# Seven products ahead of the last image's gates, its last row's sum in another order, and its last stores on two queues

## The chip, the core and the metric

The kernel runs on one core of a Trainium2 chip. A core has five engines that run their own instruction streams and wait for one another through semaphores: TensorE (PE in the profile; its weight loads are PEld), VectorE (DVE), ScalarE (ACT), GpSimd (POOL) and SyncE (SP, which here only issues DMAs). The metric is the device time of one launch in microseconds (us). Three runs of the kernel before gave 1615.23, 1620.63 and 1624.31 us, a median of 1620.63 us.

## The reference: what is computed

The input x has 4 images of 32 channels, 128 x 128, float32.

- Layer 0 makes 128 channels of 4096 points out of every image, forms the 4096-wide attention matrix of normalised points, applies it, scales by gamma and adds the input.
- Layer 1 reads the result as 4096 tokens of 128 values per image. It adds a linear attention of 8 heads (all of it folds into one 128 x 128 matrix per image), and then a mixture of experts. That last part is what matters here:

```
p = softmax(x @ router_w + router_b)        # 8 experts
top_p, top_i = top_k(p, 2);  top_p /= sum(top_p)
out = sum over the two chosen experts of top_p * (x @ expert_w[e] + expert_b[e])
t = t + out
```

## The kernel before

**Images 0 to 2** are pipelined: while one image's attention matrix is made, layer 1 of the image before runs beside it. Their tokens are sorted by expert through DRAM, so that each token meets only its two experts. **The last image (b = 3)** has nothing to hide behind, and its layer 1 is done in `last_parts` (L1419 to L1538) without sorting: every token is multiplied by all 8 expert matrices, and a gate of 8 numbers per token, 6 of them zero, weighs the results.

**Tokens.** The 4096 tokens of an image lie as 32 tiles (KT = 32) of 128 tokens; below, "row k" is tile k. `normalise` (L758, ACT) makes row k's normalised tokens, four rows are turned by four TensorE transposes into one bank of PSUM (`transpose_tokens`, L987, transposes at L995), and ACT copies the bank back (L991). Row k can only be multiplied once its group of four is turned and copied.

**Products.** `product(k, h, bank)` (L1433) multiplies row k with experts 0 to 3 (h = 0) or 4 to 7 (h = 1): one 128 x 512 float32 product, which the profile shows as two matmul records of line L1434. Its result fills one bank of PSUM. `bank` (L1423) hands out five banks in turn (two of the pool ps_e, two of ps_g, one of ps_o); a product waits until the two readers of the bank's former content are done. Three more banks belong to `psum_t` (L97), which the transposes and the temporaries of the second half's gates use.

**Weighing and adding.** For each row, `scaled_sums` (L1370, DVE, L1376) multiplies the first experts' results with their gates and adds them up in `acc`, starting from the token itself; `scaled_rows` (L1381, ACT, L1390) writes the other experts' results, each times its gate, into `tmp`. `by_scalar(k)` (L1429) says how many of the eight experts ACT takes: 6 for k < 8, 5 for k < 14, then 4. `sum_rows` (L1395) adds `tmp` into `acc` two rows at a time, on POOL; for the last pair (rows 30 and 31) on DVE, at L1398, L1399 and L1402. `store(g)` (L1404) writes four rows with four DMAs, all issued by SP.

**Order.** The streams of PE, DVE, ACT and SP are written in program order by hand (`manual_schedule`). Ahead of the row loop at L1521 stand the router of the first 16 rows (`router_rows`), its gates (`route(0)`, ending at L978), the turning of rows 0 to 3, the four products of rows 0 and 1 (L1519) and the turning of rows 4 to 7 (L1520). In the loop, row k is weighed and the two products of row k + 2 are issued. The second half's statistics and gates (`second_half`, L1473) are spread over the loop's first passes.

Of the kernel before, what the change touches and what calls it, by code (L numbers as in the profile page):

```python
# [12 lines left out]
F32 = mybir.dt.float32  # L13
BF16 = mybir.dt.bfloat16
U32 = mybir.dt.uint32
AF = mybir.ActivationFunctionType
ALU = mybir.AluOpType
# [5 lines left out]
def kernel(  # L23
# [43 lines left out]
    nc = tc.nc  # L67
    P = 128
# [7 lines left out]
    KT = 32  # L76
    S = 32
    NH, KQ, D = wk.shape
# [10 lines left out]
    work = ctx.enter_context(tc.tile_pool(name="work", bufs=2))  # L89
# [7 lines left out]
    def psum_t(name):  # L97
        return ps_t.tile([P, CH], F32, tag="pt", name=name)
# [172 lines left out]
    def tokens(ap, b):  # L271
        return ap[b].rearrange("c (s k r) w -> s r c k w", s=2, r=2)
# [445 lines left out]
    def layer1(b, st):  # L718

        alone = b == B - 1  # L720
        T = st["T"]
# [9 lines left out]
        gate = first  # L731
# [155 lines left out]
        def matrix():  # L887

            nc.vector.reciprocal(sda, rsa)
            gv = work.tile([P, NH, D + E], F32, tag="wide", name=f"gv_{b}")  # L890
            for h0 in range(0, NH, 3):
                yield
                nh = min(3, NH - h0)
                dst = gv[:, h0 : h0 + nh].rearrange("p h e -> p (h e)")

                def copy(p, dst=dst, nh=nh, h0=h0):
                    if h0 == 3:
                        nc.scalar.activation(dst, p[:, : nh * (D + E)], AF.Copy)
                    else:
                        nc.vector.tensor_copy(dst, p[:, : nh * (D + E)])  # L900

                py, done = hold(f"pgv_{b}_{h0}", copy)
                rhs = wvx[:, h0 : h0 + nh].rearrange("p h e -> p (h e)")
                nc.tensor.matmul(py[:, : nh * (D + E)], gram, rhs, start=True, stop=True)
                yield
                done()
            yield
            pm, done = hold(f"pm_{b}", lambda p: nc.vector.tensor_copy(matx[:, : D + E], p[:, : D + E]))
            for h in range(NH):
                nc.tensor.matmul(pm[:, : D + E], at_sb[:, h, :], gv[:, h, :], start=(h == 0), stop=(h == NH - 1))  # L910
            yield
            done()
# [454 lines left out]
        dst = tokens(out, b)  # L1367
        accs, tmps = {}, {}
# [23 lines left out]
                    scale=gate[:, k, e : e + 1],  # L1392
                )

        def sum_rows(kk, n=4, eng=nc.gpsimd):  # L1395
            tmp, rows = tmps[kk], accs[kk // 2][:, 2 * (kk % 2) : 2 * (kk % 2) + 2, :]
            m = n // 2
            eng.tensor_tensor(tmp[:, :, :m], tmp[:, :, :m], tmp[:, :, m : 2 * m], ALU.add)  # L1398
            eng.tensor_tensor(tmp[:, :, 0], tmp[:, :, 0], tmp[:, :, 1], ALU.add)  # L1399
            if n >= 5:  # L1400
                eng.tensor_tensor(rows, rows, tmp[:, :, 2 if n == 6 else 4], ALU.add)
            eng.tensor_tensor(rows, rows, tmp[:, :, 0], ALU.add)  # L1402

        def store(g):  # L1404
            for r1 in range(2):
                for s in range(2):
                    p0 = s * 64 + r1 * 32
                    nc.sync.dma_start(dst[s, r1, :, ts(g, 4), :], accs[g][p0 : p0 + 32])

        def all_parts():  # L1410
            yield from stagger([close_rows(kc) for kc in range(4)], 3)
# [7 lines left out]
        def last_parts():  # L1419

            turn = [0]

            def bank(name):  # L1423
                pools = ((ps_e, "pe"), (ps_g, "pg"), (ps_o, "po"), (ps_e, "pe"), (ps_g, "pg"))
                pool, tag = pools[turn[0] % 5]
                turn[0] += 1
                return pool.tile([P, CH], F32, tag=tag, name=name)

            def by_scalar(k):  # L1429

                return 6 if k < 8 else 5 if k < 14 else 4

            def product(k, h, bank):  # L1433
                nc.tensor.matmul(bank, xn[:, k, :D], ew_sb[:, 4 * h : 4 * h + 4, :], start=True, stop=True)  # L1434
                return bank

            for _ in matrix():
                pass

            la = fpool.tile([P, KT, 2 * E], F32, tag="F", name=f"la_{b}")  # L1440
            copies = {}

            def attended(u):
                if u >= 2:
                    copies[u] = fpool.tile([P, 8, D], F32, tag="F", name=f"pac_{b}_{u}")
                for j0 in range(0, 8, 3):
                    pa = bank(f"pat_{b}_{u}_{j0}")
                    attend_rows(u, j0, pa)
                    nj = min(3, 8 - j0)
                    pr = pa[:, : nj * (D + 2 * E)].rearrange("p (j d) -> p j d", d=D + 2 * E)  # L1450
                    if u < 2:
                        tg = T[:, 8 * u + j0 : 8 * u + j0 + nj, :]
                        nc.vector.tensor_tensor(tg, tg, pr[:, :, :D], ALU.add)
                    else:
                        nc.scalar.activation(copies[u][:, j0 : j0 + nj], pr[:, :, :D], AF.Copy)
                    nc.scalar.activation(la[:, 8 * u + j0 : 8 * u + j0 + nj, :], pr[:, :, D:], AF.Copy)

            def stats_of(u):
                bs, stats = batch_stats("f", 8 * u, 8)
                for f in stats:  # L1460
                    f()
                close_stats("f", 8 * u, 8, bs)

            attended(0)
            stats_of(0)
            transpose_rows(6)()
            transpose_rows(7)()
            attended(1)
            stats_of(1)
            attended(2)  # L1470
            attended(3)

            def second_half():  # L1473

                bs, stats = batch_stats("f", 16, 16)
                for u in (2, 3):
                    tg = T[:, ts(u, 8), :]
                    nc.vector.tensor_tensor(tg, tg, copies[u], ALU.add)
                    yield
                    for j in range(8):  # L1480
                        stats[8 * u - 16 + j]()
                        if j % 4 == 3:
                            yield
                close_stats("f", 16, 16, bs)
                yield

                temps = psum_t("gates").rearrange("p (n k e) -> p n k e", n=4, e=E)
                logits = router_rows(nc.vector, 16, 16, la[:, 16:], temps)
                next(logits)
                yield  # L1490
                yield
                for _ in logits:
                    pass
                gates = route(1, temps)
                next(gates)
                yield
                for g in range(4, 8):
                    normalise(range(4 * g, 4 * g + 4), rsf, nbo)
                    next(gates, None)
                    yield  # L1500
                    transpose_tokens(g)()
                    yield

            rest = second_half()
            logits = router_rows(nc.vector, 0, 16, la[:, :16])
            next(logits)
            normalise(range(0, 4), rsf, nbo)
            keep_running(6)
            transpose_tokens(0)()
            next(rest)  # L1510
            for _ in logits:
                pass
            gates = route(0)
            normalise(range(4, 8), rsf, nbo)
            next(gates)
            next(rest)
            for _ in gates:
                pass
            products = [product(k, h, bank(f"py_{b}_{k}_{h}")) for k in range(2) for h in range(2)]  # L1519
            transpose_tokens(1)()  # L1520
            for k in range(KT + 4):  # L1521
                if k < KT:
                    n = by_scalar(k)
                    scaled_sums(k, products[:2], 8 - n)
                    scaled_rows(k, products[:2], n)
                    products = products[2:]
                    if k + 2 < KT:
                        products += [product(k + 2, h, bank(f"py_{b}_{k + 2}_{h}")) for h in range(2)]
                if 1 <= k <= KT and k % 2 == 0:
                    sum_rows(k // 2 - 1, by_scalar(k - 2), nc.vector if k == KT else nc.gpsimd)  # L1530
                if k >= 5 and k % 4 == 1:
                    store(k // 4 - 1)
                if k < 8:
                    normalise(range(8 + k, 9 + k), rsf, nbo)
                    if k % 4 == 3:
                        transpose_tokens(2 + k // 4)()
                if k >= 1:
                    next(rest, None)  # L1538

        return SimpleNamespace(all_parts=all_parts, first_parts=first_parts, last_parts=last_parts)  # L1540


# [101 lines left out]
```

## Time and profile before

| what | value |
|---|---|
| median of three runs | 1620.63 us (1615.23 to 1624.31) |
| the profiled execution, its time | 1636.16 us |
| its span, first to last instruction | 1634.4 us |
| mean granted TensorE clock | 0.994 |
| PE busy | 1592.9 us, 97% of the span |
| ACT, DVE, POOL busy | 877.2, 940.0, 596.2 us |
| products of the last image (L1434) | 128 records, 61.5 us, from 1558.26 to 1626.5 us |
| scaled copies on ACT (L1390) | 150, from 1565.0 to 1627.7 us |
| scaled sums on DVE (L1376) | 106, from 1564.3 to 1627.2 us |
| stores of the last image (L1408) | 32 DMAs of 64 KB, all on SP's queue |

Times inside the profile count from the span's start. In a row of the timeline the first number is the start and the second the time until the end of that group of instructions; brackets tell how long the engine was idle before it and what released it. The table of stretches gives for every engine the busy time (and the number of instructions), then the granted clock of TensorE, where 1.00 is full speed.

### The profile page before, as it was taken

To read this page: it belongs to the slowest core of one execution; us is meant where nothing else is said; L and a number is where in the kernel's file an instruction comes from. 1 tells how busy PE (TensorE), PEld (TensorE's weight loads), DVE (VectorE), ACT (ScalarE), POOL (GpSimd) and SP (SyncE) were. 2 spreads that over 40 slices of the span, in tenths; PEclk is the share of its full clock that TensorE was granted. 3 is DMA by queue.
4 is the path that set the end of the run, shared out by engine and by line. 5 is a ranking of instruction groups with operands and counts; after the bars stand their busy time and mean duration, and the time that the engine had idled before them with its cause. 6 is when DMAs were issued, how large, how long until landed. Compare 5 with 4: busy or idle time off the path is not lost.

```text
span 1634.4 us, 20871 instructions
## 1 busy us (share of the span) xinstructions
PE 1592.9 (97%) x5019; PEld 830.1 (51%) x5019; DVE 940.0 (58%) x2369; ACT 877.2 (54%) x2779; POOL 596.2 (36%) x567
## 2 busy tenths in 40 slices
PE   8999999999999999999999999999999999998987
PEld 5444544455554454555554445555555455554633
DVE  5443343477686454469478445449568454444786
ACT  4555445466475544556565544556556444544386
POOL 1000000010025541546555542446556641545166
PEclk9999999999999999999999999999999999999999
DMA  5554756676769698998999699998899898884001
GB/s 169 191 204 163 222 184 230 221 237 210 183 211 283 187 240 253 286 254 227 204 250 279 218 231 282 248 276 221 219 234 278 266 238 252 230 272 126 10 14 39
DMA packets 374359, 349.07 MB, mean 214 GB/s; under 512 B 159968, under 2 KB 300768, under 8 KB 359904
## 3 DMA queue, kind: packets, MB, share of 16 engines
q1 hardware_dynamic: 339776, 308.23, 63.6%
q0 software_dynamic: 26624, 25.58, 7.7%
q10 hardware_dynamic: 7840, 13.93, 2.9%
q8 instruction: 42, 0.69, 0.2%
q14 instruction: 77, 0.63, 0.1%
HBM read 170.57 MB, written 182.32 MB: 216 GB/s over the span
## 4 chain that ended last, share of the span: by engine, by line
PE 89%; DVE 3%; DMA 3%; SPq 2%; ACT 1%; issue 1%; another core or an unknown queue 1%; POOL 0%; ACTq 0%; DVEq 0%
PE po L559 26%; PE pe L671 26%; PE pg L495 22%; PE py L1434 3%; PE pg L515 2%; PE pys L1193 2%; PE pgram L789 2%; PE pat L919 1%; PE pys L1243 1%; SPq L607 1%; PE pys L1200 1%; DMA F<-blocks 1%; SPq L1215 1%; DMA ys<-results 0%
## 5 line engine op out<-in xcount | busy, mean ns | idle before, releaser
L674 ACT ACTIVATE pr<-pe 128x512 f32<-128x512 f32 (+1 forms) x576 | 322.5, 560 | 609.4 <-PE pe L671 509.8
L559 PE MATMUL po<-pr,qT 128*128 128x512 f32 (+3 forms) x1152 | 548.3, 558 | 0.2 <-ACT o L564 0.2
L671 PE MATMUL pe<-qn,qn 128*128 128x512 f32 x896 | 458.6, 594 | 3.5 <-ACT pr L674 2.1
L495 PE MATMUL pg<-F,qT 128*128 128x512 f32 x880 | 451.8, 595 | 8.1 <-DMA F<-blocks 5.4
L482 DVE STREAM_TRANSPOSE F<-pr 128x512 f32<-128x512 f32 x440 | 305.1, 699 | 149.2 <-ACT pr L674 128.5
L559 PEld LDWEIGHTS po<-pr,qT 128*128 128x128 f32 x1152 | 216.4, 190 | 240.4 <-issue 224.1
L500 ACT ACTIVATE junk<-F 128x512 bf16<-128x512 f32 x440 | 273.0, 620 | 5.7 <-DMA F<-blocks 4.9
L1308 POOL DMA_INDIRECT acc<-ys,place x128 | 203.2, 1587 | 192.3 <-ACT pr L674 120.3
L495 PEld LDWEIGHTS pg<-F,qT 128*128 128x128 f32 x880 | 166.8, 191 | 203.8 <-issue 179.0
L1129 POOL DMA_INDIRECT xs<-xn,place x192 | 187.1, 975 | 183.4 <-ACT pr L674 111.3
L671 PEld LDWEIGHTS pe<-qn,qn 128*128 128x128 f32 x896 | 157.7, 191 | 130.1 <-issue 119.6
L504 DVE TENSOR_TENSOR o<-o,pg 128x512 f32<-128x512 f32 x110 | 75.0, 682 | 210.9 <-PE pg L495 181.0
L164 POOL TENSOR_TENSOR norm<-ss,neg_half 128x8 f32<-128x8 f32 (+1 forms) x17 | 27.0, 1586 | 311.9 <-DVE ss L296 304.4
L674 ACT ACTIVATION_READ_ACCUMULATOR pr<-pe 128x1 f32 x576 | 111.9, 194 | 0.0
L1308 POOL DMA_INDIRECT yb<-ys,place x64 | 61.2, 956 | 88.0 <-ACT pr L674 47.3
L671 PE MATMUL pe<-qn 128*128 128x512 f32 (+3 forms) x256 | 90.2, 435 | 0.7 <-ACT qn L365 0.7
L500 ACT ACTIVATION_READ_ACCUMULATOR junk<-F 128x1 f32 x440 | 84.4, 192 | 0.0
L1175 DVE TENSOR_TENSOR results<-pys,xn 128x256 f32<-128x256 f32 (+1 forms) x60 | 25.0, 416 | 82.9 <-ACT xn L1169 54.5
L164 POOL TENSOR_TENSOR rsa<-dm_a,neg_half 128x8 f32<-128x8 f32 x16 | 28.4, 1775 | 113.0 <-DVE sv_a L752 112.9
L1434 PE MATMUL py<-ew_sb,xn 128*128 128x512 f32 x128 | 61.5, 622 | 5.1 <-ACT tmp L1390 3.9
L671 PEld LDWEIGHTS pe<-qn 128*128 128x128 f32 x256 | 45.1, 191 | 38.1 <-issue 33.7
L164 POOL TENSOR_TENSOR rsf<-dm_f,neg_half 128x8 f32<-128x8 f32 (+1 forms) x15 | 26.3, 1751 | 103.6 <-DVE sv_f L752 103.6
(226 smaller groups left out, 1506.1 us busy)
## 6 DMA issues: line engine op xcount, KB each, us to landing
blocks<-F SPq DMA_DIRECT2D x110, 1024.0 KB
F<-blocks SPq DMA_DIRECT2D x220, 192.0 KB
F<-blocks SPq DMA_DIRECT2D x220, 128.0 KB
F<-blocks SPq DMA_DIRECT2D x220, 64.0 KB
below<-F SPq DMA_DIRECT2D x31, 384.0 KB
T<-in_x_dram SPq DMA_DIRECT2D x64, 128.0 KB
out_dram<-acc SPq DMA_DIRECT2D x128, 64.0 KB
xa<-in_x_dram SPq DMA_DIRECT2D x62, 128.0 KB
```

The source lines that it names most:

```text
L164: pinned(nc.gpsimd.tensor_tensor(dst, src, neg_half.to_broadcast(list(src.shape)), ALU.pow))
L482: f()
L495: nc.tensor.matmul(pg.rearrange("p (a f) -> p a f", a=4), st["qT"][i][:, ib, :], G[:, :, ib], start=(ib == 0), stop=(ib == NJ - 1),)
L500: nc.scalar.activation(junk, G[:, :, ib], AF.Copy, accum_out=st["sums"][:, NJ * i + ib, jc : jc + 1])
L504: nc.vector.tensor_tensor(st["o"][jc], st["o"][jc], pg, ALU.add)
L515: nc.tensor.matmul(out[:, :, : ib * S], st["qT"][i][:, ib, :], rows, start=(ib == 3), stop=(ib == 1))
L559: nc.tensor.matmul(row["po"][:, lo:hi], qT[blk // NJ][:, blk % NJ, :], w, start=start, stop=(row["left"] == 0))
L671: nc.tensor.matmul(pe[:, c0:], qn[jc][:, ts(j, P)], qn[i][:, c0:], start=True, stop=True)
L674: nc.scalar.activation(pr[:, c0:], pe[:, c0:], AF.Exp, accum_out=sums[:, t, i : i + 1]).ins
L1129: inst = nc.gpsimd.indirect_dma_start(xs[h], offset(place[:, i, k : k + 1]), xn[:, k, :], None)
L1308: inst = nc.gpsimd.indirect_dma_start(to, None, ys, offset(place[:, i, k : k + 1]), compute_op=op)
L1434: nc.tensor.matmul(bank, xn[:, k, :D], ew_sb[:, 4 * h : 4 * h + 4, :], start=True, stop=True)
```

## The change

Three things are changed, all in the last image's `last_parts`.

1. Seven products are issued ahead of the loop in place of four: both of rows 0, 1 and 2 and the first of row 3. Five take the banks of `bank`, the last two take banks of `psum_t`. They stand ahead of the turning of rows 4 to 7. In the loop, products are then issued so that four lie ahead of the row at hand: none at k = 0, one at k = 1, two from k = 2 on.
2. Row 31 has its own function, `last_row`. Its product of experts 4 to 7 is issued ahead of that of experts 0 to 3. ACT scales experts 4 to 7 and then 2 and 3; DVE takes experts 0 and 1 and adds up the six others. Row 30's four scaled results, which were added together with row 31's on DVE, are now added on POOL.
3. The last group's four stores are issued alternately by SP and ACT, two each.

```diff
+        def store(g, queues=(nc.sync, nc.sync)):
...
-                    nc.sync.dma_start(dst[s, r1, :, ts(g, 4), :], accs[g][p0 : p0 + 32])
+                    queues[s].dma_start(dst[s, r1, :, ts(g, 4), :], accs[g][p0 : p0 + 32])
+
+        def last_row(k, py):
+
+            acc, tmp = accs[k // 4][:, k % 4, :], tmps[k // 2][:, 1]
+            more = work.tile([P, 2, D], F32, tag="grp", name=f"more_{b}", bufs=2)
+            for e in (4, 5, 6, 7, 2, 3):
+                to = more[:, e - 2] if e < 4 else tmp[:, e - 4]
+                nc.scalar.activation(to, py[e // 4][:, ts(e % 4, D)], AF.Copy, scale=gate[:, k, e : e + 1])
+            for e in range(2):
+                nc.vector.scalar_tensor_tensor(
+                    acc, py[0][:, ts(e, D)], gate[:, k, e : e + 1], T[:, k, :] if e == 0 else acc, ALU.mult, ALU.add
+                )
+            nc.vector.tensor_tensor(tmp[:, :2], tmp[:, :2], tmp[:, 2:4], ALU.add)
+            nc.vector.tensor_tensor(tmp[:, :2], tmp[:, :2], more, ALU.add)
+            nc.vector.tensor_tensor(acc, acc, tmp[:, 0], ALU.add)
+            nc.vector.tensor_tensor(acc, acc, tmp[:, 1], ALU.add)
...
-            products = [product(k, h, bank(f"py_{b}_{k}_{h}")) for k in range(2) for h in range(2)]
+            heads = [(k, h) for k in range(KT) for h in ((0, 1) if k < KT - 1 else (1, 0))]
+
+            def make(n, alloc):
+                products.extend(product(k, h, alloc(f"py_{b}_{k}_{h}")) for k, h in heads[:n])
+                del heads[:n]
+
+            products = []
+            make(5, bank)
+            make(2, psum_t)
             transpose_tokens(1)()
             for k in range(KT + 4):
-                if k < KT:
+                if k == KT - 1:
+                    last_row(k, products[::-1])
+                elif k < KT:
                     n = by_scalar(k)
                     scaled_sums(k, products[:2], 8 - n)
                     scaled_rows(k, products[:2], n)
                     products = products[2:]
-                    if k + 2 < KT:
-                        products += [product(k + 2, h, bank(f"py_{b}_{k + 2}_{h}")) for h in range(2)]
-                if 1 <= k <= KT and k % 2 == 0:
-                    sum_rows(k // 2 - 1, by_scalar(k - 2), nc.vector if k == KT else nc.gpsimd)
+                    make(max(0, 4 - len(products)), bank)
+                if 1 <= k < KT and k % 2 == 0:
+                    sum_rows(k // 2 - 1, by_scalar(k - 2))
+                if k == KT - 2:
+                    sum_rows(k // 2, of=slice(0, 1))
                 if k >= 5 and k % 4 == 1:
-                    store(k // 4 - 1)
+                    store(k // 4 - 1, (nc.sync, nc.scalar if k > KT else nc.sync))
```

`sum_rows` takes in addition `of`, the rows of a pair that it adds. In the changed file the new lines of `last_row` are L1416 (ACT), L1418 (DVE's two scaled sums) and L1421 to L1424 (DVE's four additions); products are at L1450.

More of the change, by code (lines that the diff above doesn't have):

```diff
@@ L1393, in scaled_rows, with sum_rows @@
                 )
-        def sum_rows(kk, n=4, eng=nc.gpsimd):
-            tmp, rows = tmps[kk], accs[kk // 2][:, 2 * (kk % 2) : 2 * (kk % 2) + 2, :]
+        def sum_rows(kk, n=4, of=slice(0, 2), eng=nc.gpsimd):
+            tmp, rows = tmps[kk][:, of], accs[kk // 2][:, 2 * (kk % 2) : 2 * (kk % 2) + 2, :][:, of]
             m = n // 2
@@ L1402, in sum_rows @@
             eng.tensor_tensor(rows, rows, tmp[:, :, 0], ALU.add)
-        def store(g):
+        def store(g, queues=(nc.sync, nc.sync)):
             for r1 in range(2):
```

## The prediction

> **What bounds the kernel now.** First the page's totals and its chain of work that ended last:
>
> ```profile
> span 1634.4 us, 20871 instructions
> ...
> PE 89%; DVE 3%; DMA 3%; SPq 2%; ACT 1%; issue 1%; another core or an unknown queue 1%; POOL 0%; ACTq 0%; DVEq 0%
> ```
>
> TensorE carries 89% of the chain, but nearly all of that lies ahead of 1558 us, where the change touches nothing: the built instruction streams of the two kernels are the same up to there. What is at stake is the last 76 us. So next the chain in order of time, from 1555 us on (start, length, what):
>
> ```profile
> 1563.88 0.30 DVE first L978
> ...
> 1565.05 0.63 ACT tmp L1390 x2
> 1565.68 0.04 issue
> 1565.72 8.15 PE py L1434 x14
> 1573.87 0.45 PE ptf L995 x4
> 1574.35 0.60 ACT xn L991
> ...
> 1599.80 3.70 PE py L1434 x8
> 1603.50 0.44 PE ptf L995 x4
> 1603.94 22.60 PE py L1434 x52
> ```
>
> Three stages. From the gates (L978) to 1574 the chain is in TensorE, which stood still for 2.46 us (1563.26 to 1565.72) because its sixth product has no free bank until ACT has read the first. Up to 1600 the chain changes between ACT and TensorE: ACT needs about 1.89 us a row (its scaled copies of rows 0 to 3 begin at 1565.05, 1566.94, 1568.83, 1570.70), TensorE 2 x 0.86 = 1.72. From 1600 TensorE alone is the bound: 52 records in 22.60 us, 0.87 us a product.
>
> Then the table of stretches around the standstill (the clock is the third number from the end):
>
> ```profile
> 1563.50:1566.94 3.44, 1.22 (x3) 0.48 (x4) 3.17 (x13) 1.89 (x7) 0.00 (x0) 1.00 0.00 0
> 1566.94:1570.35 3.41, 3.41 (x5) 1.33 (x6) 2.75 (x8) 3.41 (x15) 1.64 (x1) 0.50 0.00 0
> ```
>
> TensorE was busy for 1.22 of 3.44 us, and for the next 3.41 us its clock was halved. That is why 14 records took 8.15 us where 14 x 0.43 = 6.02 would do, and why ACT waited 1.48 us for the next turned group (L991 at 1574.35).
>
> Last the timeline of the end:
>
> ```profile
> 1626.10 1.12 DVE L1376 SCALAR_TENSOR_TENSOR acc<-py,first,acc 128x128 f32<-128x128 f32 x3
> 1626.51 0.73 POOL L1402 TENSOR_TENSOR acc<-acc,tmp 128x256 f32<-128x256 f32 x1
> 1626.57 1.14 ACT L1390 ACTIVATE tmp<-py,first 128x128 f32<-128x128 f32 x4 [0.49 <-PE py L1434]
> 1627.81 0.69 DVE L1398 TENSOR_TENSOR tmp<-tmp 128x512 f32<-128x512 f32 x1 [0.59 <-ACT tmp L1390]
> 1628.53 0.43 DVE L1399 TENSOR_TENSOR tmp<-tmp 128x256 f32<-128x256 f32 x1
> 1628.99 0.43 DVE L1402 TENSOR_TENSOR acc<-acc,tmp 128x256 f32<-128x256 f32 x1
> ...
> 1629.48 1.78 SPq L1408 DMA_DIRECT2D out_dram<-acc  x4
> ```
>
> The last product ends at 1626.54, DVE at 1629.42; SP issues four stores, one each 0.36 to 0.49 us, and the span ends at 1634.35, 4.93 us after DVE.
>
> **Part 1, seven products ahead.** Three products (3 x 0.86 = 2.58 us) move into the standstill. They are not 2.58 us won, because what follows is paced by ACT. They stand ahead of the turning of rows 4 to 7, so that turning ends 2.57 us later (1564.97, not 1562.40), and its copy L991, which stands on ACT's queue ahead of the first scaled row, starts at 1565.01 in place of 1562.44. A scaled copy began 0.49 us after such a copy's start (1574.35, 1574.84). So ACT's first scaled row starts at 1565.50, not 1565.05: 0.45 late. Rows 0 to 3 find their products ready and stay 0.45 late. Row 11 is normalised behind row 3, at 1572.86 + 0.45 = 1573.31; its turning then takes 0.42 until L991 (as from 1582.65 to 1583.07), so L991 is at 1573.73 and row 4 at 1574.22 instead of 1574.84: 0.62 early.
>
> Not all of that arrives. POOL's additions run without a gap from 1568.71 to 1595 and start when ACT ends row 1, so they are 0.45 late; among them are the statistics (L164, L754) that DVE's L936 awaits: 1580.55 instead of 1580.67, 0.1 early. Behind L936 on DVE stand the second half's gates and row 9's sums, and ACT's row 9 follows DVE's (1585.05, right after DVE's 1585.02). L936 took 1677 ns where its neighbour L938 took 299, because POOL's L1398 ran just then; if it slips in ahead of POOL, DVE wins 1.4 us and the 0.62 passes. Bounds 0.1 and 0.62; I take 0.4 early. From 1600 on TensorE passes a shift on as it is.
>
> Here a rule speaks. The Trainium skill (TensorE: Matmul & The Clock Gate, section "Why this matters for your kernels") asks for no TensorE gaps over about 3 us, as one idle window brings half the clock. By it a gap of 2.46 us costs nothing; then row 4 of before would have started at 1572.86 + 0.42 + 0.49 = 1573.77, and the change loses the 0.45. The row above shows half the clock after a window that held 2.2 us of idleness, so I follow the row. But windows are not tied to the kernel's start as far as the trace tells, and other runs may miss it: this is the third rival below. The standstill doesn't vanish either: after row 5's products TensorE has no bank and no turned rows from about 1571 to 1573.3. A halved clock then would find ACT two rows behind TensorE and cost an estimated 0.2 us.
>
> **Part 2, the last row.** TensorE does the same work; only the order of its last two products changes. ACT does six copies instead of four: the first four can start at once behind row 30's (1625.95, as their product ends at 1625.7), and at 0.255 us each plus the last one's 0.38 all six end at 1627.6. DVE keeps two of its four scaled sums. But both engines read the same bank, and in this kernel one then waits for the other: ACT's first copy at 1565.05 came just behind DVE's sum, and the built stream has the first L1418 waiting for ACT as well as TensorE. So L1418 starts at about 1627.70, not 1626.57; on DVE the four additions queue behind it, then both pairs of stores. Two sums of 0.386 end at 1628.47; L1421 and L1422 (128x256, 0.43 and 0.03 for the wait) at 1629.39; L1423 and L1424 (128x128, 0.32 by L961 and its like) at 1630.03. Against 1629.42 that is 0.6 later. Row 30's addition on POOL (three steps of estimated 0.8, 0.5, 0.5 behind L1402's end at 1627.2) ends at about 1629.0, hidden behind DVE. It can hold L1421 up, as L1398 held L936: 0 to 0.46. I take 0.2. Part 2: +0.8, between +0.3 (were the wait harmless) and +1.1.
>
> **Part 3, two queues.** SP's last issue begins 1.33 us after its first; with two each it begins 0.36 after. So the last landing is at most 0.97 earlier. ACT has nothing queued behind its two stores. While four stores ran, the 16 DMA engines were about half busy in slices of 1 us (135 GB/s), so two streams fit; if not quite, an estimated 0.4 remains. ACT's issues took 0.33 to 0.86 us elsewhere. I take 0.95; bounds 0 (if something else ends the span, next rival) and 0.97.
>
> **Sum.** -0.4 + 0.8 - 0.95 = -0.55 us on an execution of 1636.16 us. The profiled one is 15.5 us (1%) above the median; a difference this small carries over as it is: 1620.63 - 0.55 = 1620.1 us.
>
> **Rivals.**
>
> *GpSimd's closing drain ends the span (slower).* At L1639 the engines close:
>
> ```profile
> L1639 POOLq DRAIN  x3: 51/107/7065, 1626.5 to 1634.1; - x3
> L1639 SPq DRAIN  x3: 7/7/7, 1632.8 to 1633.8; - x3
> ```
>
> SP has seen its stores land at 1632.84, but GpSimd's first drain, begun at 1626.47, lasts 7.065 us, to 1633.54, and only then does the common end go on, with 0.82 us left. If the drain costs a fixed 6.3 us after GpSimd's last addition (1627.23), the stores aren't the end at all, and part 2 moves that addition to 1629.0 - 0.4 = 1628.6: +1.4 us, 1622.0. It decides as soon as GpSimd's last addition ends less than 6.3 us before SP has seen its stores land. Against it: the other two drains took 0.05 and 0.11 us. That speaks for a drain that waits for the stores, and then part 3 counts.
>
> *Everything passes (faster).* 3 x 0.86 = 2.58 us of TensorE, all of the 0.95, and part 2 free: -3.5, 1617.1. Against it: ACT's 1.89 us a row.
>
> *The halved clock isn't there in timed runs.* Then part 1 is +0.45: +0.45 + 0.8 - 0.95 = +0.3, 1620.9. It is also what remains if the products ahead do nothing but delay the turning.
>
> **How the numbers follow.** The forecast 45%, GpSimd's drain 27%, no halved clock 20%, all passes 8%. They span 1617.1 to 1622.0, so a measurement, which can tell about 0.5% (8 us) from no change, will hardly see any of them. No mechanism in this profile reaches 8 us, as all that is touched is 76 us, in which TensorE is busy for 64. What widens the range is the scatter of the runs themselves, 1615.23 to 1624.31: about 4.5 us down and 3.7 up around the median, and I let the cases' ends widen it: 1614.5 to 1625.5. Faster by over 0.5%: 0.04; within: 0.92; slower: 0.04.
>
> **What would show it.** Part 1: no standstill at 1563 to 1565.7, ACT's first scaled row some 0.45 later after L978, row 4 earlier; if row 4 is over 1 us earlier or not at all, the step is wrong. Part 2: L1418 starting behind ACT's last copy, DVE's end 3.3 to 3.6 us behind the last product (2.9 before). Part 3: ACT and SP issuing side by side. The rival: GpSimd's drain still ending about 6.3 us after its last addition. A time outside the range would mean that something ahead of 1558 us has moved.

## The result, and the profile after

| | before | changed |
|---|---|---|
| median | 1620.18 us (22 runs, 1615.23 to 1624.31) | 1623.37 us (22 runs, 1617.58 to 1626.17) |
| ratio, 95% interval | | 1.0021 [1.0011, 1.0031]: +3.4 us [+1.8, +5.0] |
| profiled execution (its span) | 1636.16 us (1634.4) | 1619.99 us (1618.2) |

The change costs about 3.4 us. The forecast was -0.55 us, with 1614.5 to 1625.5 for the time: the time lies in the range, the sign is wrong. The profiled execution of the changed kernel is 16 us shorter than that of before. That comes from ahead of the gates, where the built streams are the same (L978 ends at 1564.18 before and 1546.87 after, 17.31 us earlier), so the two traces are compared by distances. The stretch from L978's end to the last product's end is called the head below, what follows the last product the tail. The head went from 62.35 to 61.72 us, the tail (to the span's end) from 7.82 to 9.62.

First the page's span and chain of the changed kernel, to be held against the first fence of the prediction:

```profile
span 1618.2 us, 20874 instructions
...
DVE 0%; ACT 0%; issue 0%
```

TensorE's 89% have gone, not because TensorE does less but because the chain loses its trail: in order of time it now begins at 1609.16 with ACT's last two copies and ends with DVE's L1424 at 1612.02. In both kernels it stops at DVE's last addition, whose result the last stores carry. It names neither the stores nor what really comes last: that is in the closing drains (the DRAIN instructions at the end of each engine's stream), here the changed kernel's (instructions of one line; count, then shortest/mean/longest in ns, then from when to when):

```profile
L1666 POOLq DRAIN  x3: 51/107/6850, 1610.5 to 1617.9; - x3
L1666 SPq DRAIN  x3: 7/7/7, 1614.8 to 1617.6; - x3
```

SP has seen its stores land at 1614.82. GpSimd's first drain goes on from 1610.54 to 1617.39, 2.57 us longer, and the span ends 0.82 us behind it. In before SP was done 0.69 ahead of the drain's end. The timeline of the changed kernel's end shows what the drain follows:

```profile
1608.56 0.72 POOL L1402 TENSOR_TENSOR acc<-acc,tmp 128x256 f32<-128x256 f32 x1
...
1609.71 0.35 DVE L1418 SCALAR_TENSOR_TENSOR acc<-py,first,T 128x128 f32<-128x128 f32 x1 [2.15 <-ACT more L1416]
...
1610.58 0.51 POOL L1402 TENSOR_TENSOR acc<-acc,tmp 128x128 f32<-128x128 f32 x1
...
1611.73 0.29 DVE L1424 TENSOR_TENSOR acc<-acc,tmp 128x128 f32<-128x128 f32 x1
1612.10 0.85 ACTq L1408 DMA_DIRECT2D out_dram<-acc  x2
```

GpSimd's last addition (the second L1402 here, row 30's) ends at 1611.09, and 1617.39 is 6.30 us later. Before, it ended at 1627.23 and its drain at 1633.54: 6.30 again. Relative to the last product GpSimd's last addition moved from 0.71 to 2.50, and the span's end moved with it by the same 1.80 us. L1418 waits for ACT, as forecast, but that wait is not on the path.

The head of the changed kernel, from its timeline:

```profile
1540.96 6.28 PE L1450 MATMUL py<-ew_sb,xn 128*128 128x512 f32 x14 [0.69 <-ACT xn L991]
1547.71 0.60 ACT L991 ACTIVATE xn<-ptf 128x512 f32<-128x512 f32 x1 [5.07 <-PE ptf L995]
1548.20 1.65 ACT L1390 ACTIVATE tmp<-py,first 128x128 f32<-128x128 f32 x6
```

The 14 records are the seven products, all at the whole clock. ACT's first scaled row starts 1.33 us after L978's end (0.87 before), row 4 10.05 after it (10.66 before). In this execution no clock was halved in the head.

### The profile page after: what moved, and what is told of

Same layout as the page of the kernel before. It is cut to its first block, busy times and chain, and to the rows that moved or that the text cites. A ratio compares the mean times of both kernels' runs of the same rounds, so it can differ in the third digit from the quotient of the medians.

```text
span 1618.2 us, 20874 instructions
## 1 busy us (share of the span) xinstructions
PE 1584.7 (98%) x5019; PEld 825.5 (51%) x5019; DVE 936.9 (58%) x2368; ACT 878.1 (54%) x2781; POOL 598.2 (37%) x570
## 5 line engine op out<-in xcount | busy, mean ns | idle before, releaser
L1450 PE MATMUL py<-ew_sb,xn 128*128 128x512 f32 x128 | 59.8, 608 | 3.8 <-ACT tmp L1390 2.6
```

## The experiments

Two theories of the tail: the drain theory (the span ends 0.82 us after GpSimd's drain, which ends 6.30 after its last addition) against the stores theory, on which the forecast was built. Two theories of part 1: it costs or gains by where the halved clock falls, or its cost is fixed. Each of the 14 kernels was compared with before on the same chip; before's median was 1619.25 to 1639.21 us in these comparisons, so only ratios are compared across them. First all the results; the profile's columns follow in the next table.

| run | ratio to before, 95% interval | in us |
|---|---|---|
| e1 part 1 alone | 1.0006 [0.9995, 1.0016] | +1.0 [-0.8, +2.6] |
| e2 part 2 alone | 1.0003 [0.9992, 1.0013] | +0.5 [-1.3, +2.1] |
| e3 part 3 alone | 0.9998 [0.9987, 1.0009] | -0.3 [-2.1, +1.5] |
| e4 change, row 30 on DVE | 1.0005 [0.9990, 1.0020] | +0.8 [-1.6, +3.2] |
| e5 change, turning first | 1.0008 [0.9992, 1.0023] | +1.3 [-1.3, +3.8] |
| e6 before, late addition | 1.0020 [1.0004, 1.0035] | +3.3 [+0.7, +5.7] |
| e7 early end of GpSimd, two queues | 1.0007 [0.9985, 1.0029] | +1.1 [-2.5, +4.8] |
| e8 ordered | 1.0000 [0.9979, 1.0021] | 0.0 [-3.4, +3.4] |
| e9 ordered, second | 0.9996 [0.9982, 1.0010] | -0.7 [-2.9, +1.6] |
| e10 seven, no spare turns | 0.9998 [0.9984, 1.0013] | -0.3 [-2.6, +2.1] |
| e11 before, no spare turns | 0.9997 [0.9983, 1.0010] | -0.5 [-2.8, +1.6] |
| e12 ordered, third | 1.0022 [1.0015, 1.0030] | +3.6 [+2.4, +4.9] |
| e13 the change again | 1.0021 [1.0007, 1.0035] | +3.4 [+1.1, +5.7] |
| e14 parts 2 and 3 | 1.0006 [0.9999, 1.0012] | +1.0 [-0.2, +1.9] |

What each profiled execution shows, in us. The first three columns count from L978's end (start of a halved clock of 3.41 us in the head, or none; ACT's first scaled row; the last product's end, which is the head). The last four count from the last product's end.

| kernel | halved from | first scaled row | head | GpSimd's last addition ends | its drain ends | SP: stores landed | span ends |
|---|---|---|---|---|---|---|---|
| before | 2.76 | 0.87 | 62.35 | 0.71 | 7.01 | 6.31 | 7.82 |
| changed | none | 1.33 | 61.72 | 2.50 | 8.80 | 6.24 | 9.62 |
| e1 | -5.75 | 3.04 | 63.43 | 0.70 | 7.01 | 6.31 | 7.82 |
| e2 | 2.55 | 0.88 | 62.37 | 2.50 | 8.81 | 6.83 | 9.62 |
| e3 | -5.50 | 0.88 | 61.27 | 0.70 | 7.01 | 5.73 | 7.82 |
| e4 | -4.98, 12.08 | 3.04 | 64.64 | 0.76 | 7.07 | 6.15 | 7.88 |
| e5 | 10.16 | 0.87 | 62.36 | 2.51 | 8.81 | 6.26 | 9.63 |
| e6 | none | 0.87 | 61.27 | 3.30 | 9.60 | 6.67 | 10.41 |
| e7 | 2.89 | 0.87 | 62.35 | -2.73 | 3.57 | 5.67 | 6.48 |
| e8 | none | 0.87 | 61.32 | 0.92 | 7.22 | 6.41 | 8.04 |
| e9 | 9.84 | 0.87 | 62.37 | 0.92 | 7.22 | 6.14 | 8.04 |
| e10 | none | 1.34 | 61.78 | 0.71 | 7.01 | 6.31 | 7.83 |
| e11 | 2.74 | 0.87 | 62.37 | 0.70 | 7.00 | 6.30 | 7.82 |
| e12 | 8.87 | 0.88 | 61.58 | 2.73 | 9.03 | 6.94 | 9.85 |
| e13 | none | 1.35 | 61.79 | 2.51 | 8.81 | 6.27 | 9.63 |
| e14 | none | 0.88 | 61.32 | 2.51 | 8.82 | 6.27 | 9.63 |

### Each part alone: e1, e2, e3

e1, the seven products on before (before's order of the last row):

```diff
-            products = [product(k, h, bank(f"py_{b}_{k}_{h}")) for k in range(2) for h in range(2)]
+            make(5, bank)
+            make(2, psum_t)
```

> Part 1 alone: seven products ahead, the end as before. If a halved clock after the standstill is the rule in the runs of before, L978's end to the last product's end is about 61.7 us (62.37 in before's trace) and the time is 0.4 to 0.7 us below before's. If before's halved clock is an exception, the timed difference is +0.2 to +0.5 us (row 0 starts 0.45 late and nothing is won back). In both, GpSimd's drain ends 6.3 us after its last addition.

GpSimd's drain ended 6.3 us after its last addition, as expected. Neither head came: it was longer, 63.43. The timed +1.0, with its interval from -0.8 to +2.6, rules out neither forecast. The table of stretches of e1, around the start of its products (PE's busy time first; the clock third from the end):

```profile
1537.99:1541.40 3.41, 2.28 (x13) 1.28 (x12) 3.11 (x10) 2.99 (x10) 2.68 (x3) 1.00 0.00 0
1541.40:1544.81 3.41, 3.41 (x5) 1.35 (x6) 3.13 (x14) 1.54 (x5) 0.00 (x0) 0.50 0.00 0
```

Here the halved clock lies on the seven products themselves. The timeline of e1 shows what that does:

```profile
1541.26 7.97 PE L1434 MATMUL py<-ew_sb,xn 128*128 128x512 f32 x14 [0.69 <-ACT xn L991]
...
1549.70 0.60 ACT L991 ACTIVATE xn<-ptf 128x512 f32<-128x512 f32 x1 [6.77 <-PE ptf L995]
1550.20 1.13 ACT L1390 ACTIVATE tmp<-py,first 128x128 f32<-128x128 f32 x4
```

The 14 records take 7.97 us, not 6.28. L991 waits for the turning behind them, and ACT's first scaled row waits behind L991: 3.04 after L978's end in place of 1.33.

e2, the changed kernel with four products ahead and `store(k // 4 - 1)` on SP alone:

```diff
-            make(5, bank)
-            make(2, psum_t)
+            make(4, bank)
```

> Part 2 alone: four products ahead, all stores on SP. Theory 'GpSimd's drain ends the span': its last addition ends about 2.5 us after the last product (0.69 before), the drain 6.3 us later, so +1.8 us on before. Theory 'the stores end it': DVE ends 0.55 later, so about +0.6 us. The head is before's, so its trace also shows once more whether the clock halves after the standstill.

The trace is the drain theory's to the digit: GpSimd's last addition 1.80 later, the drain 1.80 later, the span's end 1.80 later, though the stores landed only 0.52 later. The timed runs, +0.5 with an interval up to +2.1, fit both theories.

e3, before with the last four stores divided:

```diff
-                    store(k // 4 - 1)
+                    store(k // 4 - 1, (nc.sync, nc.scalar if k > KT else nc.sync))
```

> Part 3 alone: the last four stores on two queues. Theory 'GpSimd's drain ends the span': 0 us, the stores land about 0.6 to 0.9 earlier and the drain still ends 6.3 us after GpSimd's last addition. Theory 'the stores end it': -0.95 us. Another look at before's head and its clock.

```profile
L1639 POOLq DRAIN  x3: 51/107/7063, 1606.7 to 1614.3; - x3
L1639 SPq DRAIN  x3: 7/7/7, 1612.4 to 1614.0; - x3
```

The stores land 0.58 us earlier (5.73 after the last product, 6.31 before), and the drain ends 7.01 after it, as in before: the two queues work and buy nothing. Timed, the forecast's -0.95 is still inside the interval; the trace decides. e3's trace bears on the head, too: the halved clock met its first products like e1's, yet its head was as short as any, 61.27 (e6 has the same). With four products ahead, L991 comes 1.7 us later than usual and is still 0.9 ahead of the first scaled row, so the halved clock is hidden.

### Moving GpSimd's last addition: e4, e6, e7

e4, the change with row 30 added up on DVE:

```diff
-                    sum_rows(k // 2, of=slice(0, 1))
+                    sum_rows(k // 2, of=slice(0, 1), eng=nc.vector)
```

> The change with row 30's scaled copies added up on DVE instead of GpSimd, in the time in which DVE waits for ACT's last copies. Theory 'GpSimd's drain ends the span': GpSimd's last addition is again that of rows 28 and 29, 0.7 us after the last product instead of 2.5, so 1.8 us below the changed kernel, unless the stores now land last (then 1.0 to 1.8). Theory 'the stores end it': 0 to +0.5 against the changed kernel, as DVE has three more additions.

GpSimd's last addition is back at 0.76, and the tail at 7.88: 1.74 us of the change's 1.80 are undone by one instruction stream. DVE did not end later (3.33 after the last product against 3.44), as it added up row 30 in the time in which it would have waited for ACT. Timed, its +0.8 is 2.6 us below the changed kernel's +3.4, but the intervals overlap.

e6, before with the last addition of rows 30 and 31 on GpSimd:

```diff
-            eng.tensor_tensor(rows, rows, tmp[:, :, 0], ALU.add)
+            nc.gpsimd.tensor_tensor(rows, rows, tmp[:, :, 0], ALU.add)
```

> Before, with one instruction moved: the last addition of rows 30 and 31 is on GpSimd instead of DVE. Theory 'GpSimd's drain ends the span': GpSimd's last addition ends 2.2 us later than before, the drain 6.3 us after it, so +2.2 to +2.5 us. Theory 'the stores end it': only the addition's own difference, +0.3 us.

```profile
L1639 POOLq DRAIN  x3: 51/107/7050, 1635.8 to 1643.4; - x3
L1639 SPq DRAIN  x3: 7/7/7, 1639.9 to 1643.1; - x3
```

One addition of 0.72 us on the other engine put the tail up by 2.59 us, and the runs show +3.3 [+0.7, +5.7]. The stores landed only 0.36 later. The stores theory falls.

e7, two queues, and GpSimd's three additions of rows 28 and 29 left out (those scaled copies are missing from the output's sums):

```diff
-                if 1 <= k <= KT and k % 2 == 0:
+                if 1 <= k <= KT and k % 2 == 0 and k != KT - 2:
```

> Before with two queues for the last stores, and GpSimd's three additions of rows 28 and 29 left out, so that its last addition is that of rows 26 and 27, some 3.4 us earlier (what is left out: the scaled copies of two rows of the sum). Theory 'GpSimd's drain ends the span until it is early enough': SP sees its stores land 5.7 us after the last product, the drain ends before that, and the span ends about 6.5 after the last product instead of 7.82: -1.3 us. Theory 'the drain waits for the stores, 6.3 is chance': the drain still ends 0.7 to 1.4 after SP has seen them land.

```profile
L1639 POOLq DRAIN  x3: 51/107/7063, 1622.8 to 1632.5; - x3
L1639 SPq DRAIN  x3: 7/7/7, 1631.9 to 1632.2; - x3
```

GpSimd's first drain is as long as ever, 1622.803 + 7.063 = 1629.87, 6.30 after its last addition, but now SP comes last, at 1631.97, and the tail is 6.48. So the drain does not wait for the stores. The end is the later of the two, and only here do the two queues count. The timed runs could not see the 1.3 us (interval -2.5 to +4.8).

### The head: e5, e10, e11

e5, the change with the turning ahead of the three added products:

```diff
-            make(5, bank)
+            make(4, bank)
+            transpose_tokens(1)()
+            make(1, bank)
             make(2, psum_t)
-            transpose_tokens(1)()
```

> The change with the turning of rows 4 to 7 put back ahead of the three added products. Theory 'the products are late for the turning' (they delay L991 by 1.7 us where the clock is whole and by 3.4 us where it is halved): L991 is back ahead of L978's end, the first scaled row starts 0.88 after L978's end, row 4 about 9.6 after it, L978's end to the last product's end is 61.2 to 61.4 us whatever the clock does (61.7 to 64.6 in the kernels with seven products so far, 61.3 or 62.4 in those with four). The end is the changed kernel's, 9.6 us from the last product to the span's end. In time 0.5 to 2.5 us below the changed kernel. Rival 'the added products themselves cost': no gain.

L991 is back at 1.73 ahead of L978's end, and the first scaled row at 0.87, in e5 and, within 0.01, in the three ordered versions. (In before L991 stood at 1.74 ahead; the added products had delayed it by 2.58 us in the changed kernel and by 4.29 in e1, not by the 1.7 and 3.4 stated above.) Row 4 is at 9.60: the forecast's delay of 0.45 came from the order alone. The promise "61.2 to 61.4 whatever the clock does" failed. In e5 and e9 a halved clock came later, from about 10 us after L978's end, behind a stretch of 3.41 us in which TensorE was busy for 1.52 us (e5) and 1.75 (e9), and the heads are 62.36 and 62.37. The standstill had moved; its price had not gone.

e10 and e11 leave out `keep_running(6)` ahead of the turning of rows 0 to 3 (spare turns of TensorE that feed nothing), with seven products and with four:

```diff
-            keep_running(6)
             transpose_tokens(0)()
```

> Seven products alone, and TensorE's six spare turns left out that stand ahead of the turning of rows 0 to 3, about 9 us before L978's end; they feed nothing. Theory 'where the clock's windows lie decides what seven products cost': without them a window with little work ahead of the first product is met in most executions, the clock is halved during the seven products, the first scaled row starts 3.04 after L978's end and L978 to the last product is 63.4 or more. In time +1.5 to +2.5 us on before. Rival 'the halved clock comes and goes by chance, whatever TensorE did before': as seven products alone, +0.5 to +1.

> Before without the six spare turns. Theory 'where the clock's windows lie': the clock is halved during the first products, where four of them have 2.46 us of slack, so the first scaled row starts 0.87 after L978's end, no other halving follows, and L978 to the last product is 61.3: 0 to -1.1 us against before, and 2.1 us less than seven products without spare turns. Rival 'by chance': 61.3 or 62.4, no difference to before.

Both miss. I had meant to force the halved clock on the first products; in neither trace did it fall there. e10 had none (61.78), e11 had it after the standstill (62.37), and in time neither differs from before. So taking away 0.82 us of spare turns does not decide it, and e10 and e11 can't tell the two theories of part 1 apart. Where the halved stretches lie in all the traces says more; that follows below, with the rule on the gap.

### The pieces in another order: e8, e9, e12

All three have e5's turning and row 30 on DVE. e8 adds up rows 28 and 29 one by one on GpSimd and puts DVE's two scaled sums ahead of ACT's copies of the same bank, with ACT's loop as a helper:

```diff
-            for e in (4, 5, 6, 7, 2, 3):
+            copies((4, 5, 6, 7))
             for e in range(2):
                 nc.vector.scalar_tensor_tensor(
...
                 )
+            copies((2, 3))
```

e9 goes back to ACT's six copies first and adds one by one from row 26 on, e12 from row 20 on. This is e12's edit; in e8 the two bounds are KT - 2 and KT - 4, in e9 KT - 4 and KT - 6:

```diff
-                if 1 <= k < KT and k % 2 == 0:
+                if 1 <= k < KT - 10 and k % 2 == 0:
                     sum_rows(k // 2 - 1, by_scalar(k - 2))
+                if KT - 12 <= k < KT - 2:
+                    sum_rows(k // 2, of=slice(k % 2, k % 2 + 1))
```

> The change with three things put in another order: the turning ahead of the three added products; GpSimd's additions of rows 28 and 29 row by row, so that the last one ends about 0.4 us ahead of the last product's end, with row 30's on DVE; in the last row DVE's two scaled sums ahead of ACT's copies of the same bank. By the drain theory the span ends 6.6 to 6.8 us after the last product (7.82 before, 9.6 changed), by the theory of the turning 61.3 from L978 to the last product: together 1.0 to 2.2 us below before and 3 to 5 below the changed kernel. By the theory that the stores end it: about -1.0 on before, 0 to -1 on the changed kernel.

> As the ordered version, with two more changes: GpSimd adds up row by row from row 26 on (in the ordered version rows 26 and 27 were still a pair, and GpSimd ended 0.92 after the last product), and the last row as in the changed kernel (ACT's six copies first). By the drain theory GpSimd's last addition ends 0.4 to 0.7 ahead of the last product's end, the drain 5.6 to 5.9 after it, SP sees its stores land 5.6 to 5.9 after it, and the span ends 6.4 to 6.8 after it (7.82 before). L978 to the last product 61.3 or 62.4. In time 1 to 2 us below before.

> The second ordered version with GpSimd adding up row by row from row 20 on instead of 26, so that it is not a row behind ACT when the end comes (in the second ordered version it began row 29 1.3 us after ACT's copies, and its last addition ended 0.92 after the last product). By the drain theory GpSimd's last addition ends 0.3 to 0.5 ahead of the last product's end and the span ends 6.5 to 6.8 after it (7.82 before, 9.62 changed). In time -1.0 to -1.8 us on before, 2.5 to 4.5 below the changed kernel.

None reached its 6.4 to 6.8 for the tail: 8.04, 8.04 and 9.85. The drain again came 6.30 after the last addition; wrong was where I put that. Three additions for one row take 0.73, 0.46 and 0.46 and, with the gaps, one row in 1.75 us; for a pair 1.27, 0.73 and 0.73. TensorE delivers a row in 1.74. One by one, GpSimd never catches up, and in e12 ACT waits for it:

```profile
1606.45 2.31 ACT L1390 ACTIVATE tmp<-py,first 128x128 f32<-128x128 f32 x8 [1.13 <-POOL acc L1402]
1609.96 1.14 ACT L1390 ACTIVATE tmp<-py,first 128x128 f32<-128x128 f32 x4 [1.20 <-POOL acc L1402]
```

e8 and e9 can't be told from before; e12 loses 3.6 us [+2.4, +4.9]. Of that its tail explains 2.03, and its head nothing; the rest, about 0.4 us at the least, stays open. No version was measurably faster than before.

### The change once more, with and without part 1: e13, e14

e14 is the changed kernel with `make(4, bank)` for the seven products; e13 is the changed kernel, on the same chip.

> The changed kernel once more, beside e14. Theory 'part 2 costs 1.8 us by GpSimd's drain, part 1 costs by where the clock's windows lie': the span ends 9.62 after the last product; L978 to the last product is 61.7 or 61.8 where no halved clock meets the seven products, 63.4 or more where one does. In time +1.2 to +4 us on before. Rival 'all of the loss is part 2's': +1.8, as e14.

> The change without part 1 (four products ahead, the last row and the two queues as changed). By the drain theory +1.8 us on before, with 9.62 from the last product to the span's end; L978 to the last product as before (61.3 or 62.4). Rival 'the stores end it': -0.4.

e13 repeats the loss, +3.4. e14 has +1.0, not clear of zero. By these values part 1 costs 2.4 us; the intervals of the two overlap, and e1, part 1 alone, had +1.0. The tails of both are 9.63.

## Why the prediction was wrong

**The step that failed** is in the rival on the drain: "That speaks for a drain that waits for the stores, and then part 3 counts." The reason given, that the other two drains took 0.05 and 0.11 us, carries nothing. Between the first drain and those two GpSimd runs no addition. All 16 traces have the first drain ending 6.30 us, within 0.01, after GpSimd's last addition, whether that is 3.30 after the last product (e6) or 2.73 ahead of it (e7), and whether the stores land before or after. In before the stores were done 0.69 us too early to matter, so the forecast read the path off the wrong engine.

**Part 3**, -0.95 in the sum: measured 0. The landing comes 0.58 earlier (e3), hidden behind the drain.

**Part 2**, +0.8: measured +1.80 in the trace, for another reason than given. The forecast's picture of DVE is right: L1418 behind ACT's last copy, DVE's end 3.44 after the last product (2.89 before, forecast 3.3 to 3.6). But that path has slack. What counts is row 30's addition on GpSimd, which the forecast called "hidden behind DVE". It had put its end at 1629.0, which is 1.77 later than before's last addition; 1.80 it was. The price stood in the rival, whose sum took 0.4 off for part 1.

**Part 1**, -0.4. Where no halved clock meets the products, the working holds closely: first scaled row 0.46 late (0.45 said), row 4 0.61 early against before's trace (0.62 said), and all of that arrived at the last product (61.72 against 62.35), where the forecast let 0.4 of it pass. Its upper bound came about as it had said, by L936 (from the view of that line, before and changed; shortest/median/longest in ns):

```profile
L936 DVE TENSOR_TENSOR gates<-nbf,srw x1: 1677/1677/1677, 1580.7 to 1580.7; 128x128 f32<-128x128 f32 x1
L936 DVE TENSOR_TENSOR gates<-nbf,srw x1: 299/299/299, 1563.4 to 1563.4; 128x128 f32<-128x128 f32 x1
```

Two things were missing. Four of seven traces with four products had the halved clock after the standstill (62.4), three had not (61.3), so the gain is there in part of the executions only; against the others seven products lose 0.45, what the third rival has for part 1. And the halved clock can fall on the first products instead. With four ahead that costs nothing (e3), with seven the head is 2.16 us longer (e1 63.43 against e3 61.27), as the turning and L991 stand behind all seven. Over the traces, seven products ahead of the turning have a mean head of 62.67 (five traces), four 61.90 (seven traces; e10 and e11 counted in): +0.8 where the forecast had -0.4. This is a mean of few traces.

Two smaller terms were mis-sized. The forecast put the 14 records' 8.15 us down to the halved clock alone (6.02 without it); with the whole clock they took 6.91 (e14) and 6.90 (e6), so the halved clock is 1.24 of those 2.13 us. And a halved clock after the moved standstill, estimated at 0.2 us, went with a head 1.21 us longer in e4 than in e1, about 1.05 longer in e5 and e9 than in e8, and 0.26 longer in e12, where L936 took 0.29 us and not the 1.52 to 1.71 of those three.

**The rule of the Trainium skill** (TensorE: Matmul & The Clock Gate, section "Why this matters for your kernels"), which asks for no TensorE gaps over about 3 us and so lets 2.46 us pass, would have given +0.45 for part 1. Four traces of the head with four products have half the clock after this gap (before, e2, e7, e11), two with the same gap have not (e6, e14). Here the row was right that such a gap can cost, and wrong as a forecast of every execution.

The traces show what separates these six. Within each trace, all halved stretches start whole multiples of 3.41 us apart, so the trace can be divided into windows of that length. In before, e2, e7 and e11 one window holds so much of the standstill that TensorE is busy for 0.99 to 1.34 us of it, and the next window is halved. In e6 and e14 the edge of a window cuts the standstill, and neither part was enough (two neighbouring windows of e6, then of e14; TensorE's busy time first, clock third from the end):

```profile
1568.32:1571.73 3.41, 2.76 (x10) 1.15 (x8) 3.07 (x13) 0.60 (x1) 0.00 (x0) 1.00 0.00 0
1571.73:1575.15 3.42, 1.62 (x4) 0.59 (x4) 3.21 (x12) 2.30 (x9) 0.00 (x0) 1.00 0.00 0
...
1545.82:1549.24 3.42, 1.59 (x7) 0.63 (x5) 3.04 (x13) 0.65 (x2) 0.00 (x0) 1.00 0.00 0
1549.24:1552.65 3.41, 2.78 (x6) 0.89 (x6) 3.30 (x11) 3.41 (x14) 0.00 (x0) 1.00 0.00 0
```

The halved clock on the first products goes by the same edges: a window ends 5.75, 5.50 and 4.98 us ahead of L978's end in e1, e3 and e4, and in none of the other 13 traces does one end between 5.91 (e14) and 4.85 (e13) ahead of it. So what a kernel pays here depends on where the edges lie, and that differed between executions of the same stream. If they lie anywhere with equal chance, the halved clock meets the seven products for edges in 0.77 to 1.06 of every 3.41 us, an estimated 23 to 31% of the executions.

**The sum** from the traces: +0.8 for part 1, +1.8 for part 2, 0 for part 3 make +2.6, inside the measured +1.8 to +5.0. How it divides is known less well from the timed runs. They give part 1 +1.0 (e1) or +2.4 (e13 against e14), part 2 +0.5 (e2), and parts 2 and 3 +1.0 (e14), whose interval only just holds the trace's 1.8. How often the halved clock meets the seven products in timed runs was not measured, so part 1's size stays open within e1's interval, -0.8 to +2.6 us.

## What to carry to other kernels

Before shortening what comes ahead of a kernel's end, look at the last rows of the trace, the closing drains too, and find which engine arrives last; the chain of waits stopped at DVE's last addition and never showed GpSimd's drain. Work handed to an engine because it is idle is not free if that engine has a fixed time to pay after its last instruction. Work put into a standstill belongs behind whatever stands on the path next (here the turning), since all that exceeds the slack there is paid: of the 2.58 us by which three products delayed the turning, 0.45 at the whole clock, and 2.16 where a halved clock had used up the slack.

## What was not expected of the hardware

- GpSimd's closing drain ends 6.30 us after its last addition in all 16 traces, and the span ends 0.82 behind that when it is the last (0.81 in e6). DVE's longest drain was 0.33 in the changed kernel, that of TensorE's weight loads 2.60.
- The halved clock lasted 3.41 us each time it fell in the head, but lay in another place from one execution to the next: on the first products, after the standstill, 9 to 12 us after L978's end, or nowhere. With each of the 16 traces divided into windows as above (about 7600 in all), half the clock followed on all 55 windows in which the trace counts TensorE busy for at most 1.43 us, on 16 of some 110 with 1.44 to 2.42, and on none with more. In between the busy time doesn't decide it: 9 to 12 us after L978's end it was halved after 1.75 us (e9) and not after 1.74 (e8). What does was not found.
- Adding up rows one by one costs GpSimd 1.65 us busy a row, in pairs 1.37.
